# One core of Trainium2: zero rows, token stores and slot weights of a mixture of experts, and when a graph layer's first rows are read

## The chip, the core and the metric

The kernel runs on one core of one Trainium2 chip. The metric is device time in microseconds (us), as the median of several executions; lower is better. Engine names are those of the profile: PE is TensorE's matmul, PEld its weight load, DVE is VectorE, ACT is ScalarE, POOL is GpSimd, SP is SyncE, which here only issues transfers. A name with q behind it (SPq) stands for the transfers that this engine issues.

## The reference

There are 3327 rows `x` of 256 floats and a 3327 x 3327 adjacency matrix of zeros and ones, made at random with about 1% ones. Four residual steps follow one another, all in float32, each on layer-normalised rows:

```python
x = x + gnn(layernorm(x), adj)    # D^-1/2 (adj + I) D^-1/2 @ standardised(x @ W.T + b)
x = x + moe(layernorm(x))         # below
x = x + gat(layernorm(x), adj)    # softmax over neighbours of leaky_relu(src_i + dst_j), @ (x @ W)
x = x + heads(layernorm(x))       # 4 heads, 4 query experts each, causal attention, gate, small FFN

def moe(tokens):
    probs = softmax(tokens @ router_w.T)
    rw, re = top_k(probs, 2); rw = rw / rw.sum()
    out = tokens
    for e in range(8):
        h = gelu(tokens @ w1[e] + b1[e])          # exact gelu
        out = out + combine[:, e] * (h @ w2[e] + b2[e])
    return out
```

The change lies in `moe` and in the beginning of `gat`.

## The kernel before

Rows are held in 26 tiles of 128 (the number of rows, padded, is NP = 3328). `x` stays in SBUF. Nearly all instructions go through a wrapper, `InOrder`, that keeps on each engine the order in which the program writes them; L60 in the profile is that wrapper's line, so instructions are told apart by tile names. No scheduler moves them: where an instruction stands in a loop is where it stands in its engine's queue. Each engine runs its queue in order and stands at an instruction until what it needs is there.

**First graph layer, `graph0` (L158).** Adjacency panels `pan` are loaded by SyncE and multiplied with `y`. First all panels for row tiles 0 to 15, then row tiles 16 to 25 one after another. During the latter, pieces of the experts' routing run beside them. They are Python generators: `step` (L31) advances each of them to its next `yield`, and its argument `small` says whether a `yield 0` ends the step or only a `yield 1`.

**Routing, `Experts` (L1263).** Each token row is worked on twice, by its two experts. `route(tiles)` normalises rows into `tok` (128 x 258: 256 values, the row's index into the results and its first expert), finds the experts, works out a place for each copy of a row, and stores the copies with `put` (L1578): an indirect transfer that GpSimd issues, one 128-row tile per instruction, into the DRAM tensor `places`, where each expert has a stretch. `table(last)` (L1485) makes from the counts, for 59 slots of 128 rows (`SLOTS`), the first row in `places` (`row_i`), the expert (`exp_i`) and the bias. Row tiles 0 to 21 (`EARLY` = 22) are routed within `graph0`, and 37 slots (`SURE`) can be filled from them alone; their table is made there too. The last four tiles are routed while the first slots run; then `table(last=True)` makes the other 22 slots, and before that fills the end of each expert's stretch with a tile of zero rows: eight `put`s of `zeros` at `free_i`.

**The slots, `run` (L1591).** In turn i of a loop of 61 the queues get, in this order:

- `take(i + 4)`: SyncE reads the slot's row and expert into registers and issues two loads, `took` (128 x 258 from `places`, 129 KB) and `w1e` (the expert's first weights, 256 KB, from the input in HBM). `take(37)` waits for all `put`s, and at that turn what is left of routing and table is issued at once.
- `turn(i)`: TensorE transposes `took` into a PSUM bank (`rbank`), ScalarE copies it to `turned`, VectorE makes the index `at_to`.
- `hidden(i - 1)`: four matmuls with `w1e`, and two Gelu pieces `h` on ScalarE.
- `result(i - 2)`: two matmuls with `w2`, which is in SBUF as a whole, VectorE adds the bias into `ye`, and GpSimd stores `ye` with an indirect transfer (`put`) into the DRAM tensor `made`, at each row's own place.
- two steps of the rest: of `route` of the last four tiles, then of `table`. There a `put` of `tok` or `zeros` stands between two `yield 0`.

**Second graph layer, `graph1` (L445).** Its head is a loop of 26 + 6 turns. A tile's turn sequence is: `fetch` loads its two results of `made` (`g`), `joined` adds them with their weights to `x` (VectorE), then `norm`, `turn`, `project` and `keep` with lags of 2 to 5 turns bring `wh` and the destination terms `dst`. Beside it the first four row tiles of the adjacency are loaded in two halves each (`ar`, 128 x 1664 floats, 832 KB), ScalarE takes their signs (`sg`, bf16), and VectorE takes a maximum over `sg` and `dst` (`top`). The second part of `top` runs at the end of the loop, when the last `dst` are there. After it come the blocks of four row tiles (`rows`, exponentials on ScalarE, `masked`, matmuls into `acc`), and then `heads` (L745), which takes the last two thirds of the time.

Of the kernel before, what the change touches and what calls it, by code (L numbers as in the profile page):

```python
# [100 lines left out]
class Net:  # L101
# [342 lines left out]

    def graph1(self, xs, made):  # L445
# [5 lines left out]
        with ExitStack() as ctx:  # L451
            one = ctx.enter_context(tc.tile_pool(name="g1", bufs=1))
            rowp = ctx.enter_context(tc.tile_pool(name="g1row", bufs=4))
# [16 lines left out]
            tops, bcast, rows_, signs = {}, {}, {}, {}  # L470

            def load(t, h):

                rows_[t, h] = rowp.tile([P, HP], F32, tag="ar", name="ar1")
                nc.sync.dma_start(out=rows_[t, h], in_=a["adj"][ts(t, P), ts(h, HP)])

            def sign(t, h):
                signs[t, h] = rowp.tile([P, HP], BF16, tag="sg", name="sg")
                nc.scalar.activation(signs[t, h], rows_.pop((t, h)), AF.Sign)
# [85 lines left out]
            for k in range(NT + 6):  # L565
                if k + 6 < NT:
                    fetch(k + 6)

                for t in range(4):
                    if k == 4 + 2 * t:  # L570
                        load(t, 0)
                    if k == 11 + 2 * t:
                        load(t, 1)
                for lag, work in ((0, joined), (2, norm), (3, turn), (4, project), (5, keep)):
                    if 0 <= k - lag < NT:
                        work(k - lag)
                for t in range(4):
                    if k == 10 + 2 * t:
                        sign(t, 0)
                    if k == 20 + 2 * t:  # L580
                        sign(t, 1)
                    if k == 18 + 2 * t:
                        top(t, 0, PARTS[0])
                    if k == 28 + t:
                        top(t, 1, PARTS[0])
# [677 lines left out]
class Experts:  # L1263
# [15 lines left out]
    def __init__(self, ctx, net, dram, keep):  # L1279
# [3 lines left out]
        one = self.one = ctx.enter_context(self.tc.tile_pool(name="moe", bufs=1))  # L1283
        self.s = ctx.enter_context(self.tc.tile_pool(name="moes", bufs=8))
# [46 lines left out]
        self.puts, self.results = [], []  # L1331

    def open(self, nc):
# [5 lines left out]
        pool = self.ctx.enter_context(self.tc.tile_pool(name="mow", bufs=1, side="right"))  # L1339
        self.w2 = pool.tile([P, NE, 2, D], F32, name="w2")  # L1340
        self.b2 = pool.tile([P, NE, D], F32, name="b2")
        nc.scalar.dma_start(
            out=self.w2.rearrange("p e k f -> p (e k) f"),
            in_=a["w2"].rearrange("e (k p) f -> p (e k) f", p=P),
        )
# [16 lines left out]
    def route(self, tiles):  # L1362
# [214 lines left out]

    def put(self, nc, at, rows, to=None, group="places", puts=None):  # L1578
# [8 lines left out]
        self.tc.declare_no_dep(made.ins, group=group, reason="rows apart")  # L1587
        self.tc.add_to_no_dep_group(group, made.ins)
        (self.puts if puts is None else puts).append(made.ins.name)

    def run(self):  # L1591
        net, tc, S = self.net, self.tc, self.SLOTS
        nc = self.nc
        with ExitStack() as ctx:
# [5 lines left out]
            def take(i):  # L1600
# [4 lines left out]
                w = first[i] = wk.tile([P, 2, D], F32, tag="w", name="w1e", bufs=7)  # L1605
                nc.sync.dma_start(
                    out=w,
                    in_=self.a["w1"][ds(e, 1), :, :].rearrange("o (k p) f -> p (o k) f", p=P),
                )
                if 0 < i < self.SURE:  # L1610

                    tc.declare_no_dep(made.ins, group="places", reason="rows apart")
                    tc.add_to_no_dep_group("places", made.ins)
# [47 lines left out]
            def result(i):  # L1661
# [9 lines left out]
                y = wk.tile([P, D], F32, tag="y", name="ye", bufs=10)  # L1671
# [10 lines left out]
            rest = [chain(self.route(range(self.EARLY, NT)), self.table(last=True))]  # L1682
            for i in range(S + 2):
                if i + 4 == self.SURE:
                    while rest:
                        step(rest)
                if i + 4 < S:
                    take(i + 4)
# [6 lines left out]
                for _ in range(2):  # L1695
                    step(rest, small=True)


@with_exitstack
def tile_adj_ffn_d2(ctx: ExitStack, tc: tile.TileContext, a: dict, out: bass.AP):  # L1700
# [5 lines left out]
    with tc.tile_pool(name="feat", bufs=1) as fp:  # L1706
# [88 lines left out]
```

## Time and profile before

| what | value |
|---|---|
| median of 3 runs | 3145.96 us (3137.69, 3145.96, 3151.72) |
| the profiled execution | 3139.96 us, its span 3138.3 us |
| busy over the span | PE 88%, DVE 80%, ACT 53%, POOL 28% |
| 0 to 392 us | first graph layer with routing of tiles 0 to 21 |
| 392 to 547 us | the 59 slots: PE 131.94 of 155 us, granted clock 0.93, DMA share 0.73, 215 GB/s |
| 547 to 622 us | head of the second graph layer: PE 53.34, DVE 57.27, ACT 50.29, POOL 46.57 of 75 us |
| 622 to 1000 us | its blocks: DVE 339.85 of 378 us |
| 1000 to 3138 us | heads: DVE 1900.23 and PE 1885.18 of 2138 us |

A row of the profile's timeline gives the start in us, the duration, the engine, the operation with the tile that it writes and those that it reads, and in brackets the idle time of the engine just before it with what ended it. "issue" in such a bracket is time in which nothing that the profile shows was waited for. The page's chain of waits follows the work that ended last back from the end, and gives each engine's share of it. The windows give, for a stretch of time, each engine's busy time, TensorE's granted clock as a part of full speed, and how busy the 16 DMA engines were. Two of the DMA queues matter here: q1 holds SyncE's transfers, q0 the indirect ones of GpSimd.

### The profile page before, as it was taken

The page shows a single profiled execution, that of the slowest core. Times are in us where ns is not written, and L with a number is a line of the kernel's source. Part 1 is how long each engine was busy: PE and PEld are TensorE (multiplying, and loading weights), DVE is VectorE, ACT ScalarE, POOL GpSimd, SP SyncE. Part 2 cuts the span into 40 slices and gives each one's busy share as a digit, 9 for nine tenths or more (in the row PEclk, how much of TensorE's full clock was granted, in tenths as well). Part 3 has the DMA queues.
Part 4 walks back from the last instruction along what each step waited for, and adds up shares of the span by engine and source line. Part 5 has one row for each costly group of instructions (what it writes and reads, how often), then busy time and mean ns, then how long its engine had stood idle before and what let it go on. Part 6 is the DMA issues. An engine that isn't in the chain of part 4 may idle for free.

```text
span 3138.3 us, 126690 instructions
## 1 busy us (share of the span) xinstructions
PE 2760.8 (88%) x54254; PEld 2025.1 (65%) x54254; DVE 2495.9 (80%) x6166; ACT 1666.3 (53%) x4541; POOL 892.9 (28%) x1216
## 2 busy tenths in 40 slices
PE   7999988798896878989998998899998889999884
PEld 6888877577775656666666665556665556656553
DVE  5104533799994768989999999899999899999994
ACT  6410043755553545656666665566655656565653
POOL 6432554511122453423332222121112111111112
PEclk9999989899997878999999999999999999999997
DMA  9994476777742323334333333343433333333331
GB/s 373 356 272 145 157 232 195 267 249 246 286 168 80 80 59 90 98 85 111 106 99 100 110 104 104 96 107 105 110 102 103 104 104 112 113 104 104 112 104 54
DMA packets 262914, 447.71 MB, mean 143 GB/s; under 512 B 58800, under 2 KB 171696, under 8 KB 262224
## 3 DMA queue, kind: packets, MB, share of 16 engines
q1 hardware_dynamic: 247632, 415.71, 44.0%
q0 software_dynamic: 6960, 19.08, 1.6%
q8 instruction: 428, 7.01, 0.9%
q10 hardware_dynamic: 7760, 4.82, 0.5%
q14 instruction: 134, 1.10, 0.1%
HBM read 406.74 MB, written 25.88 MB: 138 GB/s over the span
## 4 chain that ended last, share of the span: by engine, by line
DVE 39%; PE 25%; issue 3%; ACT 3%; POOL 1%; DMA 1%; ACTq 0%; SPq 0%; POOLq 0%; DVEq 0%
DVE sc L60 34%; PE po L60 10%; PE pqk L60 8%; PE ptO L60 2%; ACT sc L60 2%; PE acc L60 2%; PE pq L60 1%; DVE l2mv L60 0%; PE pt L60 0%; PE psxt L60 0%; DVE l1mv L60 0%; DVE gl L60 0%; PE ph L60 0%; DVE fo L60 0%; DVE l2st L60 0%
## 5 line engine op out<-in xcount | busy, mean ns | idle before, releaser
L60 ACT ACTIVATE sc<-sc,anmax 128x512 f32<-128x512 f32 (+3 forms) x1568 | 1041.4, 671 | 125.2 <-DVE anmax L60 125.2
L60 DVE TENSOR_SCALAR_CACHE_REDUCE sc<-pqk 128x512 f32<-128x512 f32 (+3 forms) x1568 | 898.6, 627 | 111.5 <-PE pqk L60 110.1
L60 PEld LDWEIGHTS po<-sc,vr 32*64 32x64 f32 x43728 | 678.1, 134 | 377.6 <-DVE sc L60 203.6
L60 PE MATMUL po<-sc,vr 32*64 32x128 f32 x43728 | 784.2, 280 | 129.4 <-DVE sc L60 60.2
L60 PE MATMUL pqk<-kt,qt 64*128 64x512 f32 (+3 forms) x3136 | 833.7, 586 | 56.1 <-DVE fo L60 18.9
L60 DVE STREAM_TRANSPOSE sc<-sc 128x2048 f32<-128x2048 f32 (+3 forms) x392 | 815.8, 2082 | 10.9 <-ACT sc L60 10.8
L60 PEld LDWEIGHTS pqk<-kt,qt 64*128 64x128 f32 x3136 | 322.2, 189 | 296.3 <-issue 122.3
L60 PE MATMUL acc<-wh,p 128*128 128x259 f32 x1352 | 309.5, 387 | 34.5 <-DVE p L60 34.5
L60 POOL TENSOR_TENSOR ot<-ot,sxd 128x512 f32<-128x512 f32 x104 | 132.7, 1276 | 695.0 <-ACT ot L60 683.6
L60 PEld LDWEIGHTS acc<-wh,p 128*128 128x128 f32 x1352 | 254.3, 191 | 91.9 <-DVE p L60 52.2
L60 PE MATMUL acc<-y,pan 128*128 128x256 f32 x1352 | 300.7, 382 | 9.3 <-DMA pan<-in_adjt_dram 7.5
L60 ACT ACTIVATION_READ_ACCUMULATOR sc<-sc,anmax 128x1 f32 x1568 | 303.4, 193 | 0.0
L60 PEld LDWEIGHTS acc<-y,pan 128*128 128x128 f32 x1352 | 256.4, 191 | 49.0 <-issue 15.0
L60 ACT ACTIVATE u<-u,d 128x512 f32<-128x512 f32 (+1 forms) x182 | 125.2, 688 | 157.5 <-DVE u L60 157.3
L60 ACT COPY qkv<-ptO 128x256 f32<-128x256 f32 x104 | 38.7, 372 | 278.6 <-PE ptO L60 278.6
L60 DVE SCALAR_TENSOR_TENSOR u<-bc,d 128x512 f32<-128x512 f32 (+1 forms) x182 | 135.3, 744 | 0.1
L60 DVE SCALAR_TENSOR_TENSOR p<-pan,u 128x512 f32<-128x512 f32 (+1 forms) x182 | 125.9, 692 | 10.7 <-PE acc L60 5.8
L60 PE MATMUL ptO<-igw,ot 128*128 128x68 f32 x832 | 118.8, 287 | 12.9 <-DVE sc L60 6.0
L60 DVE DVE_READ_ACCUMULATOR sc<-pqk 128x1 f32 x1568 | 128.6, 82 | 0.0
L60 PEld LDWEIGHTS ptO<-igw,ot 128*128 128x128 f32 x832 | 104.2, 196 | 32.3 <-issue 21.1
L60 ACT ACTIVATE junk<-ar 128x1664 bf16<-128x1664 f32 x52 | 82.7, 1591 | 65.8 <-DMA ar<-in_adj_dram 64.6
L60 POOL TENSOR_TENSOR qkv<-qkv,gss 128x1024 f32<-128x1024 f32 x26 | 50.0, 1924 | 210.1 <-DVE gss L60 210.1
(286 smaller groups left out, 2874.7 us busy)
## 6 DMA issues: line engine op xcount, KB each, us to landing
vr<-vs SPq DMA_DIRECT2D x1248, 128.0 KB
ar<-in_adj_dram SPq DMA_DIRECT2D x104, 832.0 KB
pan<-in_adjt_dram SPq DMA_DIRECT2D x156, 256.0 KB
pan<-in_adjt_dram SPq DMA_DIRECT2D x26, 1024.0 KB
pan<-in_adjt_dram SPq DMA_DIRECT2D x20, 832.0 KB
w1e<-in_w_dram SPq DMA_DIRECT2D x59, 256.0 KB
vr<-vs SPq DMA_DIRECT2D x96, 96.0 KB
took<-places SPq DMA_DIRECT2D x59, 129.0 KB
```

The costliest lines, as they stand in the source:

```text
L60: made = make(*args, **kw)
```

## The change

- The eight tiles of zero rows are no longer indirect stores of GpSimd: SyncE reads the first row's number into a register and issues an ordinary transfer.
- The eight token tiles' copies of the last `route` go into a queue, `later`, from which every second turn takes one; what is left at the turn of `take(37)` is stored there. The `yield`s around `put` are gone, and `route` with `later` runs without the `yield 1` in its middle.
- All first weights `w1` (2 MB) are loaded to SBUF once, by ScalarE's queue, beside the first graph layer, and `w1e` of a slot is copied from there to its buffer by a transfer from SBUF to SBUF.
- The rows of the first block of the second layer are loaded by SyncE during the slots: a half of a tile in turns 0, 0, 0, 5, 10, 15, 20 and 25, after that turn's work. ScalarE takes their signs there in quarters of a half (128 x 416), one in each of four turns out of five, from turn 4 to 42. `graph1` finds them done.
- In `graph1` a small Exp on `own` is put at turn 30, before the blocks' first exponential.
- For the space, `tok` has 15 buffers instead of 18, `ye` 6 instead of 10, `w1e` 6 instead of 7, `sg` 8 of its own, and two pools move to the other side of SBUF.

```diff
@@ -442,6 +443,42 @@
         return make
+    def graph1_rows(self, ctx):
+        tc, a = self.tc, self.a
+        rowp = ctx.enter_context(tc.tile_pool(name="g1row", bufs=4))
+        HP = NP // 2
+        self.rows, self.signs = {}, {}
+        def load(nc, t, h):
+            self.rows[t, h] = rowp.tile([P, HP], F32, tag="ar", name="ar1")
+            nc.sync.dma_start(out=self.rows[t, h], in_=a["adj"][ts(t, P), ts(h, HP)])
+        def sign(nc, t, h, part=0, parts=1):
+            n = HP // parts
+            if part == 0:
+                self.signs[t, h] = rowp.tile([P, HP], BF16, tag="sg", name="sg", bufs=8)
+            nc.scalar.activation(
+                self.signs[t, h][:, ts(part, n)], self.rows[t, h][:, ts(part, n)], AF.Sign
+            )
+            if part == parts - 1:
+                del self.rows[t, h]
+        self.load_row, self.sign_row = load, sign
+        def beside(nc, i):
+            halves = [(t, h) for h in range(2) for t in range(4)]
+            for q, half in enumerate(halves):
+                if i == max(0, 5 * q - 10):
+                    load(nc, *half)
+            i -= 4
+            if i >= 0 and i // 5 < 8 and i % 5 < 4:
+                sign(nc, *halves[i // 5], i % 5, 4)
+        return beside
     def graph1(self, xs, made):
         tc, a, x = self.tc, self.a, self.x
         nc = InOrder(tc)
@@ -450,7 +487,6 @@
         PARTS = ((0, HP, HP + 9 * P, NP), (0, HP, NP))
         with ExitStack() as ctx:
             one = ctx.enter_context(tc.tile_pool(name="g1", bufs=1))
-            rowp = ctx.enter_context(tc.tile_pool(name="g1row", bufs=4))
             panp = ctx.enter_context(tc.tile_pool(name="g1pan", bufs=3))
             first = ctx.enter_context(ExitStack())
             ps = first.enter_context(tc.tile_pool(name="g1ps", bufs=2, space=PSUM))
@@ -467,16 +503,13 @@
             d2 = one.tile([P, NT], F32, name="d2")
             own = one.tile([P, NT], F32, name="own")
-            tops, bcast, rows_, signs = {}, {}, {}, {}
+            tops, bcast, signs = {}, {}, self.signs
             def load(t, h):
-
-                rows_[t, h] = rowp.tile([P, HP], F32, tag="ar", name="ar1")
-                nc.sync.dma_start(out=rows_[t, h], in_=a["adj"][ts(t, P), ts(h, HP)])
+                self.load_row(nc, t, h)
             def sign(t, h):
-                signs[t, h] = rowp.tile([P, HP], BF16, tag="sg", name="sg")
-                nc.scalar.activation(signs[t, h], rows_.pop((t, h)), AF.Sign)
+                self.sign_row(nc, t, h)
             def top(t, part, parts):
@@ -566,21 +599,16 @@
                 if k + 6 < NT:
                     fetch(k + 6)
-                for t in range(4):
-                    if k == 4 + 2 * t:
-                        load(t, 0)
-                    if k == 11 + 2 * t:
-                        load(t, 1)
                 for lag, work in ((0, joined), (2, norm), (3, turn), (4, project), (5, keep)):
                     if 0 <= k - lag < NT:
                         work(k - lag)
                 for t in range(4):
-                    if k == 10 + 2 * t:
-                        sign(t, 0)
-                    if k == 20 + 2 * t:
-                        sign(t, 1)
                     if k == 18 + 2 * t:
                         top(t, 0, PARTS[0])
+                if k == NT + 4:
+                    nc.scalar.activation(own[:, 0:1], shift, AF.Exp, scale=-1.0)
+                for t in range(4):
                     if k == 28 + t:
                         top(t, 1, PARTS[0])
             first.close()
@@ -1280,8 +1308,8 @@
-        one = self.one = ctx.enter_context(self.tc.tile_pool(name="moe", bufs=1))
-        self.s = ctx.enter_context(self.tc.tile_pool(name="moes", bufs=8))
+        one = self.one = ctx.enter_context(self.tc.tile_pool(name="moe", bufs=1, side="right"))
+        self.s = ctx.enter_context(self.tc.tile_pool(name="moes", bufs=8, side="right"))
...
-        self.puts, self.results = [], []
+        self.puts, self.results, self.later = [], [], deque()
@@ -1337,12 +1365,14 @@
+        self.w1 = pool.tile([P, NE, 2, D], F32, name="w1")
         self.w2 = pool.tile([P, NE, 2, D], F32, name="w2")
...
-        nc.scalar.dma_start(
-            out=self.w2.rearrange("p e k f -> p (e k) f"),
-            in_=a["w2"].rearrange("e (k p) f -> p (e k) f", p=P),
-        )
+        for w, v in ((self.w1, a["w1"]), (self.w2, a["w2"])):
+            nc.scalar.dma_start(
+                out=w.rearrange("p e k f -> p (e k) f"),
+                in_=v.rearrange("e (k p) f -> p (e k) f", p=P),
+            )
@@ -1359,7 +1389,8 @@
-    def route(self, tiles):
+    def route(self, tiles, later=False):
...
-            tok = s.tile([P, D + 2], F32, tag="tok", name="tok", bufs=18)
+            tok = s.tile([P, D + 2], F32, tag="tok", name="tok", bufs=15)
@@ -1475,12 +1506,14 @@
         place = s.tile([P, 4, 2], I32, tag="rplace", name="rplace", bufs=8)[:, :n, :]
         nc.vector.tensor_copy(place, at)
         for i in range(n):
-            if i == 2:
+            if i == 2 and not later:
                 yield 1
             for k in range(2):
-                yield 0
-                self.put(nc, place[:, i, k : k + 1], toks[i])
-                yield 0
+                put = partial(self.put, nc, place[:, i, k : k + 1], toks[i])
+                if later:
+                    self.later.append(put)
+                else:
+                    put()
     def table(self, last=False):
@@ -1496,7 +1529,10 @@
             nc.vector.tensor_copy(free_i, free)
             for e in range(NE):
                 yield 0
-                self.put(nc, free_i[:, e : e + 1], self.zeros[:, e, :])
+                at = nc.sync.value(free_i[0:1, e : e + 1], NE * self.ROOM - P)
+                made = nc.sync.dma_start(out=self.places[ds(at, P), :], in_=self.zeros[:, e, :])
+                self.apart(made, "places")
+                self.puts.append(made.ins.name)
                 yield 0
         _, past, tiles, first = self.narrow
...
-    def run(self):
+    def run(self, beside):
@@ -1602,15 +1641,14 @@
                 took[i] = wk.tile([P, D + 2], F32, tag="took", name="took", bufs=6)
                 made = nc.sync.dma_start(out=took[i], in_=self.places[ds(at, P), :])
                 e = nc.sync.value(exp_i[0:1, i : i + 1], NE - 1)
-                w = first[i] = wk.tile([P, 2, D], F32, tag="w", name="w1e", bufs=7)
+                w = first[i] = wk.tile([P, 2, D], F32, tag="w", name="w1e", bufs=6)
                 nc.sync.dma_start(
-                    out=w,
-                    in_=self.a["w1"][ds(e, 1), :, :].rearrange("o (k p) f -> p (o k) f", p=P),
+                    out=w.rearrange("p k f -> p (k f)"),
+                    in_=self.w1[:, ds(e, 1), :, :].rearrange("p o k f -> p (o k f)"),
                 )
@@ -1668,7 +1706,7 @@
                         self.w2[:, ds(ep, 1), f, :].rearrange("p o d -> p (o d)"),
                         start=(f == 0), stop=(f == 1),
                     )
-                y = wk.tile([P, D], F32, tag="y", name="ye", bufs=10)
+                y = wk.tile([P, D], F32, tag="y", name="ye", bufs=6)
                 nc.vector.tensor_tensor(
                     y, py[:, 0, :], self.b2[:, ds(e, 1), :].rearrange("p o d -> p (o d)"), ALU.add
                 )
@@ -1679,11 +1717,13 @@
             ready = wk.tile([P, 1], F32, name="ready")
             nc.scalar.activation(ready, self.count[:, 0:1], AF.Gelu)
-            rest = [chain(self.route(range(self.EARLY, NT)), self.table(last=True))]
+            rest = [chain(self.route(range(self.EARLY, NT), later=True), self.table(last=True))]
             for i in range(S + 2):
                 if i + 4 == self.SURE:
                     while rest:
                         step(rest)
+                    while self.later:
+                        self.later.popleft()()
                 if i + 4 < S:
                     take(i + 4)
                 if i < S:
@@ -1694,6 +1734,9 @@
                     result(i - 2)
                 for _ in range(2):
                     step(rest, small=True)
+                if self.later and i % 2:
+                    self.later.popleft()()
+                beside(nc, i)
 @with_exitstack
@@ -1708,11 +1751,12 @@
         net.x = fp.tile([P, NT, D], F32, name="x")
         weights = net.graph1_weights(fp)
-        with ExitStack() as moe:
-            experts = Experts(moe, net, dram, fp)
-            net.graph0(experts, weights)
-            experts.run()
-        net.graph1(xs, experts)
+        with ExitStack() as rows:
+            with ExitStack() as moe:
+                experts = Experts(moe, net, dram, fp)
+                net.graph0(experts, weights)
+                experts.run(net.graph1_rows(rows))
+            net.graph1(xs, experts)
     net.heads(xs, vs, out)
```

More of the change, by code (lines that the diff above doesn't have):

```diff
@@ L2 @@
 from contextlib import ExitStack
+from functools import partial
 from itertools import chain
@@ L1576, in table, with apart @@
             nc.vector.tensor_tensor(self.had, self.had, tiles, ALU.min)
+    def apart(self, made, group):
+        self.tc.declare_no_dep(made.ins, group=group, reason="rows apart")
+        self.tc.add_to_no_dep_group(group, made.ins)
     def put(self, nc, at, rows, to=None, group="places", puts=None):
@@ L1586, in put @@
         )
-        self.tc.declare_no_dep(made.ins, group=group, reason="rows apart")
-        self.tc.add_to_no_dep_group(group, made.ins)
+        self.apart(made, group)
         (self.puts if puts is None else puts).append(made.ins.name)
-    def run(self):
+    def run(self, beside):
         net, tc, S = self.net, self.tc, self.SLOTS
@@ L1604, in take @@
                 e = nc.sync.value(exp_i[0:1, i : i + 1], NE - 1)
-                w = first[i] = wk.tile([P, 2, D], F32, tag="w", name="w1e", bufs=7)
+                w = first[i] = wk.tile([P, 2, D], F32, tag="w", name="w1e", bufs=6)
                 nc.sync.dma_start(
-                    out=w,
-                    in_=self.a["w1"][ds(e, 1), :, :].rearrange("o (k p) f -> p (o k) f", p=P),
+                    out=w.rearrange("p k f -> p (k f)"),
+                    in_=self.w1[:, ds(e, 1), :, :].rearrange("p o k f -> p (o k f)"),
                 )
                 if 0 < i < self.SURE:
-                    tc.declare_no_dep(made.ins, group="places", reason="rows apart")
-                    tc.add_to_no_dep_group("places", made.ins)
+                    self.apart(made, "places")
                 if i in (0, self.SURE):
```

## The prediction

> **What bounds the kernel now.** I read the page first, then the stretch that the change touches, from 392 to 622 us, by windows, by the timelines of GpSimd, SyncE, TensorE, VectorE and ScalarE, and by the DMA queues. The page's chain says what most of the time is, and that the change cannot reach it:
>
> ```profile
> DVE 39%; PE 25%; issue 3%; ACT 3%; POOL 1%; DMA 1%; ACTq 0%; SPq 0%; POOLq 0%; DVEq 0%
> ```
>
> The third that is VectorE's `sc` (34% in the chain's list of lines) is the last stage, after 1000 us, where no instruction is added or removed. What can change is the 59 slots (first store at 402.75, last at 544.83) and the head of the second graph layer (547 to 622).
>
> ```profile
> core 0: us, PE busy (x) PEld busy (x) DVE busy (x) ACT busy (x) POOL busy (x), PEclk, DMA share, GB/s
> 400.00:420.00 20.00, 19.48 (x143) 17.97 (x143) 9.23 (x35) 11.78 (x34) 11.02 (x13) 1.00 0.82 243
> 440.00:460.00 20.00, 14.68 (x84) 12.89 (x83) 4.06 (x14) 5.67 (x19) 11.51 (x13) 0.83 0.80 230
> 460.00:480.00 20.00, 14.52 (x82) 12.73 (x81) 4.44 (x16) 5.45 (x18) 12.45 (x13) 0.87 0.74 210
> 500.00:520.00 20.00, 17.94 (x124) 15.79 (x123) 5.76 (x18) 8.70 (x27) 8.68 (x10) 1.00 0.84 259
> ```
>
> TensorE is full at both ends of the slots, and in the middle a quarter of it lies idle with a granted clock of 0.83 to 0.87, though the DMA engines move less than before. At full pace a slot takes 1.98 us, read from one `w,h` group to the next:
>
> ```profile
> 515.43 1.03 PE L60 MATMUL rbank<-w,h 128*128 x4
> 517.40 1.03 PE L60 MATMUL rbank<-w,h 128*128 x4
> ```
>
> In the middle GpSimd issues two indirect stores for each slot, 0.96 us and 0.30 us of issue each, in unbroken runs. Beside a run SyncE gets one load out per 2.14 us, where it takes 0.87 elsewhere (392.51 to 401.18 for ten), and ScalarE stands for 4.75 us:
>
> ```profile
> 461.33 0.96 POOL L60 DMA_INDIRECT made<-ye,at_to  x1 [0.30 <-issue]
> 462.59 0.96 POOL L60 DMA_INDIRECT places<-zeros,free  x1 [0.30 <-issue]
> 463.85 0.96 POOL L60 DMA_INDIRECT made<-ye,at_to  x1 [0.30 <-issue]
> 465.11 0.96 POOL L60 DMA_INDIRECT places<-zeros,free  x1 [0.30 <-issue]
> ```
> ```profile
> 460.95 0.67 SPq L60 DMA_DIRECT2D took<-places  x1
> 463.12 0.70 SPq L60 DMA_DIRECT2D w1e<-in_w_dram  x1
> 465.24 0.70 SPq L60 DMA_DIRECT2D took<-places  x1
> 467.37 0.01 SPq L60 DMA_DIRECT2D w1e<-in_w_dram  x1
> ```
>
> When the run ends (466.07) everything moves again. So this stretch is bound by the issue of indirect stores, not by bytes. In the second layer's head VectorE is the pace, and it waits three times for ScalarE:
>
> ```profile
> 583.83 1.89 DVE L60 CUSTOM_DVE_ANT_0 sg<-sg,dst 128x1664 bf16<-128x1664 bf16 x1 [2.80 <-ACT dst L60]
> 603.66 1.36 DVE L60 CUSTOM_DVE_ANT_0 sg<-sg,dst 128x1152 bf16<-128x1152 bf16 x1 [0.99 <-ACT dst L60]
> 612.14 0.27 DVE L60 TENSOR_SCALAR d<-wh 128x26 f32<-128x26 f32 x2 [3.03 <-ACT wh L60]
> ```
>
> **The change part by part**, against the profiled execution (3139.96, span 3138.3).
>
> *Fewer indirect stores (L1482, L1499).* Results 13 to 29 (VectorE's `ye` at 431.26 and 482.15) took 50.9 us for 16 slots; at 1.98 they take 31.7, so 19.2 us are at stake. Afterwards two slots hold three indirect stores: 3 x 1.26 = 3.78 us of GpSimd in 3.96 of TensorE. That fits with a pause of 0.48 per two slots (0.30 of issue and 0.18 spare); single stores leave 1.02 each and disturb nothing from 513 to 525. How much disturbance remains at 1.5 stores is not in the trace. Lower bound nothing; upper bound what unbroken runs cost: four stores from 452.38 until the next result at 458.11 are 1.43 us each, six from 436.52 until 445.27 are 1.46. 24 stores x 1.43 = 34.3, against 31.7: 2.6 left. I take 2.6, the nearer row, gain 16.6.
>
> *Zero rows on SyncE.* Eight transfers of 129 KB at 0.87 us of issue each lie in eight successive slots: SyncE then needs 3 x 0.87 = 2.61 per 1.98, and falls behind 5.0 us. Behind each zero transfer wait the next slot's loads, and behind those TensorE. They are hidden by SyncE's lead: the buffers let it run five to six slots ahead (9.9 us), less about 3 us from issue to landing. It also waits there for `free`, which VectorE makes some two slots before the first zero transfer is due: cost nothing while the lead is over 4 us. Without cover: 5.0.
>
> *The DMA engines.* From the DMA queues between 392 and 547, q1 moved 23.27 MB in 55.5% of 155 us, 270 GB/s at full duty; the second layer's head moved 9.50 MB in 93.9% of 28 us, 361 GB/s, with longer rows. An SBUF to SBUF copy of `w1e` (262 KB, 2 KB pieces) is in no row: by those two rates it takes 0.73 to 0.97 us, and I take 0.73, the rate of longer pieces. `took` 0.49, the store 9.85 MB in 16.6% over 75 = 0.34: 1.56 per slot of 1.98. An adjacency half of 0.852 MB takes 2.36 at 361 GB/s. From slot 5 one comes per five slots, 0.47 per slot: 2.03, just over the pace. Over the 16 slots with late stores that is 0.8, zeros add 8 x 0.49 = 3.9 and late stores 8 x 0.34 = 2.7: 7.4 us over, against a cover of 7. With 0.97 per copy it would be 11.2. SyncE's and the DMA's delay use the same cover: I take 3.3 us uncovered, between 0 and 9.
>
> *Three halves at once after slot 4's loads.* 3 x 2.36 = 7.1 us of transfers stand ahead of slot 5's rows; issued near 402, those land near 410, and TensorE would have wanted them at 405: 5 us. But here it loses already: results 0 to 13 took 29.7 us for 13 slots, 4.0 above pace, and 4.05 of it lies between 410.34 and 414.39. The two overlap. I take 2 us lost, between 0 and 6.
>
> *The table and the wait for all rows.* Before, the table is made in a rush at slot 33: SyncE issues no load from 479.10 to 489.37, and results 29 to 41 (482.15 to 510.29) take 28.1 for 23.8 at pace. With the yields of `put` gone the table is spread over earlier slots, so its rows are ready. Gain 4.3, bounds 0 and 4.3.
>
> *Signs.* A quarter of 1.48 us, 0.4 to 0.45, goes on ScalarE in four of five slots. ScalarE's work per slot is 0.37 + 0.62, so it fits in 1.98; it comes after both `h`, in the idle time of about 0.45 before `turned`. No cost, bound 3. ScalarE waits in it if a half has not landed, but the later halves are issued nine or more slots ahead. In the second layer 8 x 1.48 = 11.8 us leave ScalarE; what VectorE gets of it is its two waits, 2.80 + 0.99 = 3.8. The 3.03 stays, since that is the last tile's own way through GpSimd, ScalarE and TensorE. Early Exp table: the load (1.28, 621.29) lies beside VectorE's `u`, 0.2. Gain 4.0, bounds 3 and 6.
>
> *Hidden edits.* `tok` with 15 buffers: at tiles 15 to 21 the puts waited for are 18 us and more old. `ye` with 6: the last store was issued at 544.83 and all results had landed by 547.44, so under 3 us against six slots (11.9). `w1` is loaded once beside the first layer (DMA share 0.33 to 0.53 from 255 to 305). `wh`'s memset leaves the middle of the slots, where it held GpSimd for 4.44 us at a time when no store was due earlier: nothing.
>
> **A rule against the change.** The second layer's 334 GB/s over 548 to 584 at a DMA share of 0.94, beside 230 at 0.80 in the slots, show the bytes being moved from a full stage into a nearly full one. The Trainium skill, DMA: Bandwidth & Descriptors (SWDGE vs HWDGE vs iDMA), says that transfers from any issuing engine run on the same 16 DMA engines, so that another engine only saves sequencer time, usually small. By that rule the zeros' move would give only 8 x 1.26 = 10.1 us of GpSimd time, off the path, and the sum would lose most of its 16.6. The 4.75 us stall at a DMA share of 0.74 speaks against the rule's "small" here.
>
> **Sum.** 16.6 - 3.3 - 2 + 4.3 + 4.0 = 19.6: 3139.96 - 19.6 = 3120.4. The median of before stands 6.0 above its profiled execution, which would give 3126.4. I take 3123, the middle.
>
> **The rivals.** *The DMA engines take it back.* `w1e` at 0.97 and a duty that stops at 0.94 as in the head: 11.2 us of the excess, the burst at its bound of 6, only half the lead as cover: 16.6 - 8 - 6 + 4.3 + 4.0 = 11 at best, 3 if the zero transfers are uncovered too. Counted like the forecast, midway between profiled run and median (3143): 3132 to 3140, middle 3136. For it: 0.82 to 0.84 of DMA share in the best slots. Against: from 505 to 545 the table of waits gives TensorE only 1.3 us for `took`, at that share.
>
> *Slower: SyncE becomes the pace.* If the 0.48 us pause is too short to let SyncE go, the eight zero slots hold three loads at 2.14 each: 6.4 us a slot against 3.18 now, +25.8; the other eight stay at 3.18, and the table and the head give 8.3: 3143 + 25.8 - 8.3 = 3160.5, and if the profiled run's footing is not the median's, 3157 to 3163: at the edge of what can be told as slower (3161.7), over it by any of the bounds above, such as the 5.0 of the zero slots' loads. It decides where the pause is under what one load needs, 0.87; the pause is under it, so only the load's own queueing between the stores speaks against. For it: 2.14 per load in every unbroken run.
>
> *It does not do what it says*: late stores bunch at slot 33 if `put`s remain. Eight entries leave at odd slots from 15 to 29, so none remains; under 3%.
>
> **How the numbers follow.** Forecast 0.62, DMA rival 0.21, SyncE rival 0.14, bunched 0.03. A measurement of this kernel tells about 0.5% (15.7 us) from no change. The forecast's own range is 3108 (no disturbance left, no cover needed: 28 us gained, less the scatter of the runs) to 3132; nearly all of it is faster by over 0.5%. The DMA rival is within (3130.2 to 3161.7); the SyncE rival is counted as slower. With the rivals the range is 3108 to 3154. Faster 0.62, within 0.22, slower 0.16.
>
> **What would show it.** Right: TensorE at 19 of 20 and a clock near 1.00 between 440 and 480, no stand of ScalarE over 2 us, SyncE's loads without the 2.14 rhythm, no ten-microsecond hole of SyncE before slot 37's load, last store near 528, VectorE without the 2.80 before its first `sg`. Wrong: waits of TensorE for `took` between 404 and 470 (DMA), or SyncE periods over 2 us beside the zero transfers (SyncE), or signs standing ahead of `turned`.

## The result: no difference that can be measured

12 runs of the changed kernel and 12 of the kernel before have medians of 3141.21 and 3141.43 us, ratio 1.0003 (95% interval 0.9989 to 1.0018). The forecast of 3123 was wrong, and the time lies inside neither rival's sum; it is 1.2 us over the upper end of the DMA rival's. The traces say more than the totals. "Again" is a second trace of the same kernel. "0 to 13" is the time from result 0 to result 13, read from the starts of VectorE's `ye`; the other rows are read from TensorE's matmuls:

| us | before | again | after | again |
|---|---|---|---|---|
| first layer's last `acc` ends at | 390.3 | 390.4 | 393.3 | 395.6 |
| result 0 to 13 | 29.7 | 29.6 | 38.3 | 40.6 |
| 13 to 29 (zero rows, late stores) | 50.9 | 51.2 | 46.9 | 45.2 |
| 29 to 41 (table, slot 37's wait) | 28.1 | 26.8 | 23.7 | 23.7 |
| 41 to 58 | 33.5 | 33.9 | 34.3 | 35.3 |
| last result to first `acc<-wh` | 80.4 | 80.5 | 78.4 | 78.7 |
| first `pqk` (the heads begin) at | 999.3 | 1000.0 | 1002.1 | 1004.1 |
| from there to the end | 2139.0 | 2126.9 | 2133.8 | 2127.8 |

Up to the heads the two traces agree to 1 us for the kernel before and to 2 us for the changed one. (Two traces of one later kernel, `spread_dve_late` and `best_again`, are 9 us apart there, so a difference of a few us in a single trace proves little.) The heads, which no edit touches, differ by 12 us between two traces of one kernel. So steps are read from the first six rows, and totals only as medians and ratios over many runs.

Windows of the changed kernel, to be read beside those of the prediction:

```profile
core 0: us, PE busy (x) PEld busy (x) DVE busy (x) ACT busy (x) POOL busy (x), PEclk, DMA share, GB/s
400.00:420.00 20.00, 15.02 (x81) 13.55 (x81) 4.28 (x14) 7.48 (x25) 7.84 (x9) 0.73 0.94 332
440.00:460.00 20.00, 16.44 (x105) 13.69 (x103) 5.08 (x18) 9.85 (x30) 11.55 (x13) 1.00 0.79 252
460.00:480.00 20.00, 13.21 (x78) 11.62 (x79) 8.59 (x38) 5.69 (x16) 7.12 (x8) 0.83 0.84 251
500.00:520.00 20.00, 19.65 (x140) 17.85 (x139) 6.41 (x21) 11.95 (x35) 9.59 (x10) 1.00 0.76 245
```

The window at 400, full before (19.48), has a hole of 5 us, with the DMA engines at 0.94. The one at 460 is emptier than before. TensorE's timeline has the holes:

```profile
407.08 1.03 PE L61 MATMUL rbank<-w,h 128*128 x4
413.09 0.66 PE L61 MATMUL rbank<-ident,took 128*128 128x128 f32 x2 [4.98 <-DMA took<-places]
...
465.44 1.03 PE L61 MATMUL rbank<-w,h 128*128 x4
471.13 0.66 PE L61 MATMUL rbank<-ident,took 128*128 128x128 f32 x2 [4.66 <-DMA took<-places]
```

Both are waits for rows (`took`) that come late. What SyncE did ahead of each:

```profile
402.96 1.50 SPq L61 DMA_DIRECT2D ar<-in_adj_dram  x3
404.97 0.34 SPq L61 DMA_DIRECT2D took<-places  x1
...
460.24 0.36 SPq L61 DMA_DIRECT2D places<-zeros  x1
461.71 0.69 SPq L61 DMA_DIRECT2D took<-places  x1
462.51 0.49 SPq L61 DMA_DIRECT2D w1e<-w  x1
463.52 0.36 SPq L61 DMA_DIRECT2D places<-zeros  x1
463.99 0.40 SPq L61 DMA_DIRECT2D ar<-in_adj_dram  x1
465.48 0.24 SPq L61 DMA_DIRECT2D took<-places  x1
466.24 0.51 SPq L61 DMA_DIRECT2D w1e<-w  x1
467.44 0.36 SPq L61 DMA_DIRECT2D places<-zeros  x1
```

The rows of slot 5, issued at 404.97 behind three halves, land 8.0 us later; those of slots 0 to 4 landed 2.0 to 2.7 us after their issue. Beside the zero transfers one `took` follows the last after 3.8 us (461.71 to 465.48), nearly two slots of TensorE. From `took` 18 to 26 SyncE takes 32.6 us for eight slots, 4.07 each (3.76 in the second trace); TensorE's pace is 1.98. On GpSimd's queue the runs of stores are shorter, not gone:

```profile
449.67 0.96 POOL L61 DMA_INDIRECT places<-tok,rplace  x1 [0.31 <-issue]
450.94 0.96 POOL L61 DMA_INDIRECT made<-ye,at_to  x1 [0.30 <-issue]
452.20 0.96 POOL L61 DMA_INDIRECT made<-ye,at_to  x1 [0.30 <-issue]
453.47 0.96 POOL L61 DMA_INDIRECT places<-tok,rplace  x1 [0.30 <-issue]
```

When this queue pauses (468.2 to 475.9), and the zero transfers are over, a pair of SyncE's loads takes 2.04 us. How much of the slowness is the third transfer and how much the stores beside it, this row alone doesn't tell.

A longer wait than before stands in the first layer, where w1's 2 MB are loaded (issued at 180, the DMA engines full of panels until 210): TensorE waits 4.2 us for panels between 195 and 215, where it waited 1.8. And one wait is new in the second layer's head:

```profile
207.73 4.55 PE L61 MATMUL acc<-y,pan 128*128 128x256 f32 x20 [3.81 <-DMA pan<-in_adjt_dram]
```
```profile
585.56 1.89 DVE L61 CUSTOM_DVE_ANT_0 sg<-sg,dst 128x1664 bf16<-128x1664 bf16 x1 [0.19 <-ACT wh L61]
605.74 1.36 DVE L61 CUSTOM_DVE_ANT_0 sg<-sg,dst 128x1152 bf16<-128x1152 bf16 x1 [1.00 <-ACT dst L61]
612.55 0.44 DVE L61 TENSOR_SCALAR d<-wh 128x26 f32<-128x26 f32 x2 [1.36 <-ACT wh L61]
614.50 0.24 DVE L61 TENSOR_SCALAR own<-wh,shift 128x26 f32<-128x26 f32 x1 [1.51 <-ACT own L61]
```

The 2.80 ahead of the first `sg` is gone. The 0.99 is not (1.00 here), though the signs are done long before: it was never the signs. The last row's wait is new: VectorE's `own` stands behind the early Exp.

### The profile page after: what moved, and what is told of

Its sections match the earlier page's. It is cut to its first block, busy times and chain, and to the rows that moved or that the text cites. A ratio compares the mean times of both kernels' runs of the same rounds, so it can differ in the third digit from the quotient of the medians.

```text
span 3135.9 us, 126711 instructions
## 1 busy us (share of the span) xinstructions
PE 2743.8 (87%) x54254; PEld 2010.2 (64%) x54254; DVE 2497.0 (80%) x6166; ACT 1670.4 (53%) x4566; POOL 888.9 (28%) x1208
## 4 chain that ended last, share of the span: by engine, by line
DVE 38%; PE 26%; ACT 3%; issue 3%; POOL 1%; DMA 1%; ACTq 0%; DVEq 0%; POOLq 0%
DVE sc L61 32%; PE po L61 10%; PE pqk L61 9%; ACT sc L61 2%; PE acc L61 2%; PE ptO L61 2%; PE pq L61 1%; PE psxt L61 1%; DVE l2mv L61 0%; PE pt L61 0%; DVE gl L61 0%; DVE l1mv L61 0%; PE ph L61 0%; DVE fo L61 0%; PE pv L61 0%
```

## The experiments

Theories: **S**, SyncE's issue is now the pace of the slots; **D**, the bytes on the DMA engines are; **G**, GpSimd's runs of stores hold up the other engines; **W**, w1's load holds up the first layer; **P**, the early Exp holds up VectorE. **R** and **B** are about the heads and come up further down. "First query" is the first `pqk`, "the slots" the time from the first to the last result. Every row of the table is one trace; ratios are to the kernel before, with a 95% interval.

| kernel | first layer ends | 0-13 | 13-29 | 29-58 | last result to `acc<-wh` | first query |
|---|---|---|---|---|---|---|
| `rows_back` | 394.3 | 30.7 | 42.6 | 61.8 | 83.0 | 997.0 |
| `no_burst` | 395.2 | 34.7 | 47.6 | 59.9 | 78.4 | 1000.5 |
| `w1_dve` | 394.1 | 35.6 | 38.6 | 56.0 | 77.8 | 985.2 |
| `zeros_pool` | 394.5 | 44.9 | 44.8 | 58.0 | 78.7 | 1006.0 |
| `w1_hbm` | 396.0 | 38.7 | 42.7 | 56.0 | 77.7 | 997.4 |
| `w1_late` | 390.3 | 37.0 | 43.1 | 59.5 | 78.7 | 995.3 |
| `stores_only` | 390.2 | 31.0 | 40.0 | 57.1 | 82.4 | 986.1 |
| `spread_dve_late` | 390.0 | 29.3 | 33.4 | 56.0 | 79.0 | 971.1 |
| `best_again` | 392.0 | 30.5 | 38.7 | 56.0 | 79.2 | 980.2 |
| `every_third` | 390.0 | 29.3 | 32.7 | 56.9 | 79.0 | 972.6 |
| `no_preload` | 391.0 | 30.6 | 37.9 | 56.3 | 76.9 | 976.7 |
| `issue_back` | 389.9 | 31.6 | 43.1 | 56.8 | 80.0 | 986.6 |
| `bytes_back` | 391.3 | 31.5 | 41.5 | 60.2 | 79.5 | 990.6 |

**Rows and signs out of the slots** (`rows_back`: `beside(nc, i)` removed, loads and signs back in `graph1`'s loop).

> The changed kernel with the rows of the first block and their signs back in the head of the second layer. Theory S (the slots are now paced by SyncE's issue, about 2.0 to 2.1 us for the two loads of a slot, so that no lead is regained once lost): results 0 to 13 fall from 38.3 us to about 30, since no three halves stand ahead of the rows of slot 5; results 13 to 29 stay near 45 (46.9 in the changed kernel), since each of the eight zero transfers still costs SyncE a slot of 3.6 us or more; the head takes 2.6 us longer; in all 6 to 8 us faster than the changed kernel, about 3134 where that is at 3141. Theory D (the bytes on the DMA engines): 2.36 us go with each half, so 13 to 29 falls too, to 40 or less, and the whole is 11 to 13 us faster than the changed kernel, about 3129.

Ratio to before 0.9975 (0.9955 to 0.9995). 0 to 13 is back at 30.7: the halves of this stretch cost 7.6 to 9.9 us. Nearly all of it is one step, from result 2 to 3: 8.40 and 10.95 us in the two traces of the changed kernel, 1.15 here. 13 to 29 falls by 4.3, between the theories. From 29 to 58 it is 3.8 slower, with TensorE waiting 3.9 us for `took`, so the slots take 135.0 us of 143.2.

**One half every fifth turn.**

```diff
-                if i == max(0, 5 * q - 10):
+                if i == 5 * q:
...
-            i -= 4
+            i -= 8
```

> The changed kernel with one half of the rows in every fifth turn from turn 0 on (0, 5, 10, ... 35) and the signs four turns later. Theory S: results 0 to 13 at 30 to 32 us instead of 38.3; results 13 to 29 stay near 45 since the zero transfers fall into the same slots; results 29 to 41 keep 23.7 to 26; the whole 6 to 8 us faster than the changed kernel, about 3134. Theory D: the same bytes come, only later: 0 to 13 falls to 31, and what is saved there is lost after result 29, where the last halves now lie, so the whole is 0 to 3 us faster.

Ratio 0.9986 (0.9965 to 1.0007), slots 142.1 us of 143.2. Nearer to D than to S: 0 to 13 falls by 3.6 only, to 34.7, where both said 30 to 32, and 2.5 of it are lost again by result 58. With the copies on SyncE eight halves spread out cost 7.1 us against none (`rows_back`, 135.0), and the burst 8.2 to 9.8.

**First weights copied by VectorE** (in `turn`, ahead of `at_to`).

```diff
-                nc.sync.dma_start(
-                    out=w.rearrange("p k f -> p (k f)"),
-                    in_=self.w1[:, ds(e, 1), :, :].rearrange("p o k f -> p (o k f)"),
-                )
+                nc.vector.tensor_copy(
+                    w.rearrange("p k f -> p (k f)"),
+                    self.w1[:, ds(e, 1), :, :].rearrange("p o k f -> p (o k f)"),
+                )
```

> The changed kernel with each slot's first weights copied by VectorE (a 128x512 copy, 0.69 us by the head's copy of that size) instead of by a transfer of SyncE. SyncE then issues one load a slot. Theory S: the three halves still hold slot 5's rows (results 0 to 13 at 33 to 36 us), but SyncE regains its lead, and the zero slots cost it about 2.5 us where they cost 3.6 to 5.1: results 13 to 29 at 32 to 36 us instead of 46.9, the whole 13 to 18 us faster than the changed kernel, about 3126. Theory G (the indirect stores themselves, three in two slots, still hold up the other engines): 13 to 29 stays over 42, the whole under 6 us faster. Theory D predicts about what S does, since 262 KB a slot leave the transfers too; it is told from S elsewhere.

Ratio 0.9969 (0.9952 to 0.9986), slots 130.2, 13 us less. From 402 to 534 TensorE waits for no `took` at all, not even behind the burst; a copy takes 0.43 us. It waits 5.6 us for VectorE instead, where the copy stands ahead of `at_to`. 13 to 29 is 38.6, over S's bounds and under G's. The edit takes both a transfer's issue and its bytes away, so it doesn't tell S from D.

**Zero rows by GpSimd again** (`self.put(nc, free_i[:, e : e + 1], self.zeros[:, e, :])` in `table`).

> The changed kernel with the eight tiles of zero rows stored by GpSimd's indirect stores again, one a turn, the token tiles still every second turn. Theory G: GpSimd has 2.5 stores in a zero slot, in unbroken runs at 1.43 us: results 13 to 29 at 32 x 1.43 = 46 to 51 us, the whole as the changed kernel or up to 5 us slower. Theory S: SyncE has two loads in these slots instead of three, so what it saves (8 x 0.9 = 7 us) stands against the freezing; the rest as in the changed kernel: 13 to 29 at 42 to 47.

Ratio 1.0009 (0.999 to 1.0027), slots 147.7, 4.4 more than in the changed kernel. The run doesn't tell what it should: in its trace four token stores stand in one row on GpSimd's queue (440.54 to 444.33), in an unbroken run of eight with results and zeros, and results 10 to 13 take 13.8 us. It shows the price of such a run again, 8 us here, but not that of the zeros alone. From 430 to 495 TensorE waits 4.2 us for `h` and 6.5 for nothing that the profile shows, and not for `took`.

**First weights from HBM; w1 loaded at row tile 20.** These are two runs, each made from the changed kernel.

> The changed kernel with w1e loaded from HBM as before (the copy of w1 in SBUF is still loaded at the start, and not used). It moves the same bytes, in pieces of 1 KB instead of 2 KB. SyncE's pair of loads took 2.0 us in the first slots of the changed kernel and 1.74 before. Theory S: SyncE gains 0.26 us a slot where nothing else holds it: the slots (first to last result 143.2 us) take 4 to 9 us less, most of it after the burst and beside the zero transfers. Theory D: by the queues' rates the copy moves its bytes in less time than the HBM load (0.73 against 0.97 us a slot), so the slots take 0 to 8 us more. Both: the first layer still ends 3 us late.

> The changed kernel with the 2 MB of w1 loaded at row tile 20 of the first layer (near 280 us) instead of at 180.8 us. Theory W: at 180 to 210 us the DMA engines are full with panels, and TensorE's wait of 3.8 us for a panel there is this load; without it the first layer's last matmul ends near 390 as before (393.3 in the changed kernel, 394 to 395 in the four runs made from it), and the whole is 3 to 4 us faster. Rival: the 3 us are scatter of the first layer between runs: the end stays between 392 and 395, and the whole is as the changed kernel.

`w1_hbm` (ratio 1.0034, 1.0013 to 1.0055): slots 137.4, 5.8 less, as S said and D did not. `w1_late` (1.0038, 1.0024 to 1.0053): the first layer ends at 390.3, and the wait for panels in this stretch is 1.6 us instead of 4.2, so W holds. All traces bear it out: the seven with w1 loaded at 180 end the first layer at 393.3 to 396.0, the ten others at 389.9 to 392.0. In both traces the heads begin 2 and 4 us before those of the kernel before, yet the ratio is above 1. The kernel before ran at 3123.6 in the set that was taken with these two and the next two runs, at 3136, 3141 and 3142 in others: a shift of whole sets by 0.5%, whose cause is open.

**All three edits** (halves spread; copies by VectorE two slots ahead; w1 at row tile 20), then with late stores every third turn.

> Three edits together: the halves one every fifth turn, the slot's first weights copied by VectorE (0.43 us each in the run before) two slots ahead instead of by SyncE, and w1 loaded at row tile 20. Theory S with G: without the burst and with one load a slot, TensorE waits for no took; results 0 to 13 at 30 us, 13 to 29 at 37 to 39, limited by the stores in unbroken runs, 29 to 58 at 56; first to last result 124 instead of 143.2; the first layer ends near 390; with the head's 2.6 us the whole is 20 to 24 us faster than the changed kernel, about 3115 to 3119. Theory D (the halves cost their bytes wherever they are): each half still costs 1 to 2.4 us, so the slots take 132 or more and the whole gains 10 to 13.

> The kernel with the three edits, with a late store in every third turn instead of every second (six of them so, the last two at the turn of slot 37's load). Theory G: GpSimd then has four stores in three slots, 5.04 us of 5.94, and catches up after each disturbance: results 13 to 29 at 32 to 35 us instead of 37 to 39, but two stores in a row at turn 33 give back about 1.5; the whole 2 to 4 us faster than with every second turn. Rival: what is left there is not the stores' density but SyncE's third transfer or VectorE's steps for the table: no difference.

Ratios 0.997 (0.9953 to 0.9986) and 0.9967 (0.9954 to 0.998), slots 118.7 and 118.9. The windows of `spread_dve_late`:

```profile
400.00:420.00 20.00, 19.70 (x145) 18.26 (x145) 13.45 (x51) 14.13 (x43) 12.40 (x14) 1.00 0.61 192
440.00:460.00 20.00, 19.11 (x137) 17.36 (x136) 16.38 (x66) 13.16 (x38) 12.87 (x14) 1.00 0.92 282
460.00:480.00 20.00, 20.00 (x145) 18.48 (x144) 9.49 (x31) 13.51 (x39) 10.71 (x11) 1.00 0.68 219
```

TensorE is nearly full in these windows, with the same halves and the same zero transfers; 0 to 13, with three of the halves, takes 29.3, as in the kernel before. 13 to 29 came out at 33.4, better than the 37 to 39 expected. Every third turn instead of every second (32.7) makes no difference in this pair. But later traces with every second turn took 38.7 (`best_again`) and 37.9 (`no_preload`), so G's gain of 2 to 4 us is neither shown nor ruled out.

**Are 28 us given back in the heads?** The ratio showed only 9.

> The kernel before itself, for a second trace of it beside the next ones. Theory R (the last stage, which no edit touches, differs by 10 to 30 us from one execution to the next through the granted clock, and the earlier stages do not): the first query of the heads starts at 999 within 2 us, as in the first trace, and only the time after it (2139 us in that trace, 2124 to 2154 in the nine others) is another one. Rival B (what is saved early is given back by a lower clock in the last stage): the stage is shorter here, 2122 to 2130, than in the fast kernel beside it.

> The changed kernel again, beside the kernel before. Theory R: its first query comes at 1002 within 2 us, 2 to 4 later than in the kernel before, and the times agree within what the runs scatter: ratio 0.998 to 1.003. Theory B makes no difference here, since the early stages take the same time.

> The kernel with the three edits (halves spread, first weights copied by VectorE, w1 loaded late) again. Theory R: first query at 971 within 2 us, 28 us ahead of the kernel before, and the time 20 to 28 us shorter than before in the mean over the runs (ratio 0.991 to 0.994). Theory B: again only 9 to 13 us shorter (ratio 0.996 to 0.997), with a last stage 10 us and more longer than in the kernel before.

`before_again` 0.9993 (0.998 to 1.0007), `after_again` 0.9992 (0.9978 to 1.0007), `best_again` 0.9924 (0.9906 to 0.9941): 24 us are saved by the runs, and 20 until the first query by the trace (980.2 against 1000.0). B asked for 9 to 13 in the runs, so as it stood it falls. The traces alone would have spoken for it: the heads took 2126.9 us in the kernel before and 2139.5 in `best_again`. Over all traces they took 2135.1 to 2153.7 where the first query came before 991, and 2123.6 to 2139.0 where it came at 995 or later; every kernel has one or two traces, so a few us given back are not ruled out. 13 to 29 took 38.7 in this trace, 5.3 more than in the last one of the same kernel, with TensorE waiting 4.1 us for `h`. That would fit G; no run tests it.

**The stores alone** (zeros by SyncE, late stores every second turn; nothing else but the early Exp).

> Of the change only the stores: zero rows by plain transfers of SyncE, late stores every second turn, table steps spread. No copy of w1 in SBUF, w1e from HBM, rows and signs in the second layer's head. The forecast's own term by itself: results 13 to 29 at 34.3 us, 29 to 41 at 23.8, first to last result 122. Theory S: the two loads and the zero transfer still take SyncE over 2.6 us in eight slots beside the stores; the gains of the two runs that took the rows (4.3) or the copies (4.2) away add up: 13 to 29 at 38 to 39, first to last result 128 to 130; the head as before; first query 10 to 13 us ahead of the kernel before.

Ratio 0.9935 (0.9916 to 0.9953). First query 13 to 14 us ahead of before, slots 128.1, 13 to 29 at 40.0: close to what S said (10 to 13, 128 to 130, 38 to 39). SyncE still takes 28.9 us for eight slots with zero transfers, 3.61 each.

**Issue or bytes?** The edits above that helped most took both away.

> The kernel with the three edits, and in every slot one more small transfer of SyncE at a register's address (64 bytes for each of 128 partitions, from the SBUF copy of w1 into a buffer that nobody reads), with its register load; so SyncE has two transfers a slot again, and the DMA engines 8 KB more instead of 262. Theory S: the slots (first to last result 118.7 and 125.3 us without it) take 134 us or more, with waits of TensorE for took beside the zero transfers. Theory D: 119 to 127, as without it.

> The kernel with the three edits, and in every second slot one SBUF to SBUF transfer of 524 KB by SyncE at a fixed address, into a buffer that nobody reads: the bytes of the copies, with half as many transfers and no register loads. Theory S: 119 to 129 us from the first to the last result. Theory D: 134 us or more.

There is one run of each. With the issue back, the slots take 131.5 us against 118.7 to 125.3 without: 6 to 13 us, less than S asked, more than D allowed, and with TensorE waiting 3.2 us for `took` at the end of the zero transfers. `bytes_back` takes 133.1, but it doesn't add bytes alone. Its buffer `much` exists once, so SyncE stands until the last transfer into it has landed (us in total, times, longest):

```profile
SPq L61 <- DMA much<-w: 18.3, 11, 4.9
```

Its 8 to 14 us can be this held-up queue as well as the bytes, and TensorE waits for `took` only 3.0 us in it. So the price of the issue is shown, by one trace; the price of the copies' bytes stays open. That bytes can hold up rows is seen in the burst, where slot 5's rows took 8.0 us to land at a DMA share of 0.94.

**The early Exp taken out.**

> The kernel with the three edits, without the small Exp on own in the second layer's head, so that the Exp table is loaded again beside VectorE's first u. Theory P (the early Exp puts its table load, 1.28 us, and itself ahead of VectorE's own, which waits 1.5 us for it): the wait goes, the 1.28 us come back in part before the first exponential; from the last result to the first matmul on wh 77 to 78 us instead of 79.0 and 79.15. Rival: VectorE's own waits for the last wh anyway: 79 as before. In the whole time neither can be told (ratio 0.990 to 0.997).

Ratio 0.9925 (0.9901 to 0.995). VectorE's `own` follows at once, and 79.1 us from the last result to `acc<-wh` become 76.9: P holds, and the early Exp cost 2.2 us.

```profile
589.47 0.45 DVE L61 TENSOR_SCALAR d<-wh 128x26 f32<-128x26 f32 x2 [1.35 <-ACT wh L61]
589.84 0.23 DVE L61 TENSOR_SCALAR own<-wh,shift 128x26 f32<-128x26 f32 x1
```

## Why the prediction was wrong, step by step

Up to the first `acc<-wh` the forecast had 19.6 us gained, and the first pair of traces has 1.7 lost. Of these 21.3 us, 9.3 lie in results 13 to 29, 6.6 in 0 to 13, 3.0 in the first layer, 2.1 in the head.

- **Zero rows on SyncE**: the step that failed most. It priced three loads at 3 x 0.87 = 2.61 us, from a stretch where nothing else ran. They take 3.61 in `stores_only`, and 4.07 and 3.76 in the two traces of the changed kernel. Over eight slots that is 14 to 17 us over pace instead of 5.0. The cover that the prediction set against it was too small: a `took` was issued 9 us ahead of its use at slot 18 and only 3 at slots 22 to 24. So 13 to 29 lost 12.6 us against 34.3, where 3.3 were taken. The SyncE rival named the mechanism, with 6.4 per slot too much. That the remaining runs of stores are what makes a load dearer than 0.87 is likely, but no run takes them away alone.
- **Copies on chip**: priced for their bytes only, at an unchanged issue. The pair of loads takes SyncE 2.0 us instead of 1.74, more than TensorE's slot, so lead that is lost is hardly regained:

```profile
393.38 0.36 SPq L61 DMA_DIRECT2D took<-places  x1
394.25 0.60 SPq L61 DMA_DIRECT2D w1e<-w  x1
395.40 0.35 SPq L61 DMA_DIRECT2D took<-places  x1
396.35 0.52 SPq L61 DMA_DIRECT2D w1e<-w  x1
```

  From `stores_only` to `rows_back`, which adds the copies, the slots go from 128.1 to 135.0, and from slot 20 to the end `took` is issued only 2 to 4 us ahead of its use.
- **Three halves at once**: 2 taken, bounds 0 and 6. All halves of this stretch cost 7.6 to 9.9 (`rows_back`), and 3.6 to 5.9 of it came from the burst (`no_burst`). "The two overlap" was the mistake: the step of 4.05 before result 5 is there in `rows_back` too (3.75), where routing's matmuls stand between the slots; it stayed (3.71 and 3.72 in the changed kernel), and the burst's wait came on top, two steps earlier.
- **w1 hidden beside the first layer**: the DMA share was looked up at 255 to 305; the load is issued at 180, where the DMA engines are full of panels. Cost 3 us and more, where nothing was taken.
- **Fewer indirect stores**: 34.3 for results 13 to 29 was right as a mechanism. Without the other parts (`stores_only`) it gave 40.0, a gain of 10.9 of the 16.6; with the copies on VectorE 33 to 39. In the changed kernel 4.0 was left.
- **Table**: 4.3 forecast, 4.4 and 3.1 measured (28.1 and 26.8 to 23.7). Right.
- **The head**: 4.0 taken, 1.9 measured. The first wait went as forecast (2.6); the second, 0.99, had another cause; the early Exp, put down as a gain of 0.2, cost 2.2.
- **Signs** on ScalarE: hidden but for at most 2.1 us, TensorE's waits for `h` between 442 and 490. No run moves the signs alone.
- **The rule against the change** (the Trainium skill, DMA: Bandwidth & Descriptors, SWDGE vs HWDGE vs iDMA): that the transfers of all issuing engines share the DMA engines, no run here shows by itself. That the sequencer time saved is usually small is not what this case shows: `issue_back` adds 8 KB a slot and loses 6 us or more.

By stage, for the first pair of traces: first layer +3.0, 0 to 13 +8.6, 13 to 29 -4.0, 29 to 41 -4.4, 41 to 58 +0.8, head -1.9, and -0.4 between first layer and first result: 1.7 later at the first `acc<-wh` (625.85 against 624.15). The gains were real; the load on SyncE, the burst, w1's load and the early Exp took them back. With the copies on VectorE, the halves spread, w1 loaded late and no early Exp, but the zero transfers still on SyncE, the kernel is 24 us faster than before (`no_preload`, ratio 0.9925).

## What to carry to other kernels

A load moved to a queue costs that queue's issue in the stretch where it is issued, beside what disturbs it there; a price read from a quiet stretch is only its lower bound. Add up each queue's issue per turn and compare it with the pace: at 2.0 against 1.98 a queue has no slack for a further transfer. An experiment that adds bytes needs buffers enough that the queue doesn't stand for them. A transfer moved to "beside other work" is hidden or not by the window in which it is issued, not by the one in which it is needed.

## What the runs showed of the hardware

- An SBUF to SBUF transfer at a register's address was dearer to issue than the same size from HBM: 0.49 to 0.60 us on SyncE against 0.38 (392 to 403 us of both kernels), with up to 0.49 for the register load ahead of it where 0.27 was usual. It was so for 8 KB too (0.49, `issue_back`), and at a fixed address (0.47 in most rows, `bytes_back`).
- VectorE copied 128x512 floats within SBUF in 0.43 us (`w1_dve`); the same copy out of PSUM took 0.69 (`bc`, 620.90 in the kernel before).
- Two traces of the kernel before differed by 12 us in a stage of 2.1 ms; from 1160 to 1320 us the granted clock was 0.93 in the longer one and 0.98 in the other.
